# Graph attention on one core: batch 0's self features by seven block products, value blocks built in two groups of batches

## The chip, the cores and the metric

The kernel runs on one core of a Trainium2 chip. A core has five engines that run side by side, each with an instruction stream of its own: TensorE (PE, matrix products, with its weight loads shown as PEld), VectorE (DVE), ScalarE (ACT), GpSimd (POOL) and SyncE (SP), which in this kernel only issues DMAs. Transfers run on sixteen DMA engines. The metric is the device time of one execution in microseconds (us); lower is better.

## The reference

A graph attention layer, all in float32: B = 16 batches, N = 512 nodes, F = 512 features, H = 16 heads of 32 features, L = 11 edge labels, and only the first NG = 20 nodes of each batch serve as keys. What is computed, cut to its core:

```
row_zero  = v.sum(-1) == 0
q_exp     = where(row_zero, 0, q)                       # q: one vector per batch
self_feat = concat([v, q_exp]) @ W_self.T + b_self
output    = self_feat
for d in 0, 1:
    A    = adj if d == 0 else adj with its node axes swapped;  A = A[:, :, :20, :]
    cond = A.sum(-1);   vb = A @ w_bias + b_bias
    kv   = self_feat[:, :20]
    aff  = (self_feat @ Wq.T + bq) . (kv @ Wk.T + bk) / sqrt(32)       # per head
    aff  = where(cond > 0, aff, -9e15) + vb
    output += (softmax(aff) @ kv) @ Wout.T + bout                      # per head
result = v + relu(output)
```

## The kernel before, in words

Features lie on the partitions: a batch's input `x` is 4 chunks of 128 features x 512 nodes, and so is `sf`, its self feature. The query weights are folded into the keys, so that a batch's scores are one product of `sf` with a key tile `g` (4 chunks x 608 columns). Key 0 of each batch is taken off the others, so 19 key differences are left.

**Setup (to 91.4 us).** It makes the key rows, and then the key tiles of all 16 batches in 22 bursts of matmuls (`keys`, L674), n = 0 to 21. ACT and DVE empty each burst's two pairs of banks (L689, L691), and SP stores the keys in DRAM (`g_d`, `g1_d`). Behind the bursts from n = 4 on, PE does what the string `plan` says, one group of letters a burst: b and c are bias terms, v and w the value products (`values`, L649), n the flags of nodes whose row is not zero for batches 0 and 1, and s a step of batch 0's self feature. `values` copies its product to SBUF and stores it by POOL's DMAs in `vw_d` in DRAM.

**Batch 0's self feature before** (`self_feat`, L205) is a direct product: four quarters, each 4 x 2 x 4 matmul instructions over the four chunks of `x`. Three of the quarters are in the setup's plan, the fourth stands in the main loop between the scores of tiles 0 and 1.

**The self features of batches 1 to 15** are made while the batch before runs, by seven products of half-size blocks (`product`, L282, 32 matmul records each) instead of the eight of the direct way. They need sums of weight blocks (`weight_sums`, once, POOL) and sums of `x` blocks (`x_sum`, four a batch, POOL, L247). Products 1, 6, 7 and 4 add up in the banks `ps_a`; after each, DVE takes the banks' state to SBUF together with the flagged query term `nz` x `qw` (`partial`, L289). Products 2, 5 and 3 go to `ps_d` and `ps_c`, and DVE adds them to a partial (`joined`). A product that writes into `ps_a` must wait for the partial before it. In time: products 1 and 2 in tile 2 of the batch before, 6, 7 and 5 in tile 3, 4 and 3 in the batch's own tile 0.

**Main loop.** 16 batches of 4 tiles (`nt`) of 128 nodes. A tile: `scores` (PE, L365, into one of two pairs of banks `ps_s`), `weigh` (DVE: add the mask L379, maximum L383, subtract L387), `expo` (ACT, L392), `normal` (DVE sums L415 and L416, POOL multiply L417), `turn` (DVE transpose L424). `attend` (L435), `finish`, `residual` (L449) and `store` (L454) of batch b-1 run in tiles 2 and 3 of batch b. The masks come from the edge labels `adj`: `mask_mul` (ACT, L317), `mask_count` (DVE L322), `mask_sum` (DVE L328), `mask_spread` (ACT, L337), `full_add` (POOL, L344).

**The flags `nz` of batches 2 to 15.** `load_xn` (L111) brings the batch's rows two batches ahead, ACT sums them in tile 3 (`row_sum`, L169, four instructions), POOL compares with zero and a DMA stores 2 KB to `nz_d` (`row_mask`, L173 and L174), and a DMA spreads them over all partitions (`load_nz`, L178). `partial` is their user.

**Value blocks.** `attend` wants each batch's values as block-diagonal tiles `vd`, read from `bd_d` in DRAM (`load_values`, L139). `bd_d` (2 MB) is filled with zeros by one DMA (`clear_blocks`, batch 0, tile 1), and the values are copied into it from `vw_d` by twelve DMAs of 128-byte pieces (`blocks`, L162, batch 0, tile 2), each for all 16 batches.

**What sets the order.** The whole program is under a manual schedule: each engine runs its instructions in the order in which the code issues them, and a tile's buffers and semaphores make an engine wait. SP is one queue in order: a DMA that waits holds back all DMAs issued after it. `behind(dma, instruction)` ties a DMA to the end of an instruction of an engine, so that it is not issued earlier. Eight semaphores serve SP's DMAs in turn, so that a DMA also waits for the landing of the eighth before it.

## Time and profile before

| | us |
|---|---|
| three runs | 586.54, 587.45, 587.57 |
| median | 587.45 |
| the profiled execution | 586.05 |
| its span, first to last instruction | 583.9 |
| PE busy | 575.7 |
| DVE, ACT, POOL busy | 489.0, 395.6, 384.9 |
| main loop's first scores start | 91.38 |
| batch 1's, batch 2's first scores start | 122.48, 152.96 |

The rows are read in this way. A row of the costliest groups has line, engine, operation, output and input with their shapes, the number of instructions, then busy time and the mean of one in ns, and behind the bar's second part the idle time of the engine just before them with what ended most of it. A row of the chain or of the list of single instructions begins with the start and the duration in us. A row of waits has engine, tile and line, what was waited for, then the sum, the number and the longest. In a table by windows the columns are the stretch, its length, the busy time of PE, PEld, DVE, ACT and POOL with the number of instructions, the granted clock of PE, the busy share of the DMA engines and GB/s. A row on DMAs has the tiles, their number, the KB of each and the median us from issue to landing. SPq is SP's queue: start and duration of the issue.

### The profile page before, as it was taken

The numbers are of one execution on the slowest core, as the hardware profiler recorded it, in microseconds if no ns is written. First come the engines' busy times: TensorE is split into PE (matmuls) and PEld (weight loads), VectorE is DVE, ScalarE is ACT, GpSimd is POOL, SyncE is SP. The second block draws the span as 40 slices with busy tenths as digits, with TensorE's granted clock in tenths as the row PEclk, the third lists the DMA queues.
The fourth block names the chain that finished last, engine by engine and source line by source line (L and its number), as shares of the span: only waits on it lengthen the run. The fifth ranks groups of instructions, "written<-read, shape, count | busy, mean of one in ns | idle before, by whom it ended". The sixth has DMA issues, their size and how long they took to land.

```text
span 583.9 us, 30310 instructions
## 1 busy us (share of the span) xinstructions
PE 575.7 (99%) x13184; PEld 437.0 (75%) x13184; DVE 489.0 (84%) x783; ACT 395.6 (68%) x1162; POOL 384.9 (66%) x351
## 2 busy tenths in 40 slices
PE   9999999999999999999999999999999999999996
PEld 6654547887878787877878787787887878787873
DVE  0485565889898989899999999898989898989895
ACT  1334644586877777868686868687786877777671
POOL 2405663648778685858586777686868677776775
PEclk9999999999999999999999999999999999999999
DMA  8999899857766675757576767676676765664404
GB/s 303 388 407 311 331 377 320 273 123 213 209 197 196 185 214 169 217 167 217 168 214 171 214 171 212 177 199 188 199 202 187 199 198 172 199 199 114 144 15 146
DMA packets 103220, 124.14 MB, mean 213 GB/s; under 512 B 21712, under 2 KB 71920, under 8 KB 101040
## 3 DMA queue, kind: packets, MB, share of 16 engines
q1 hardware_dynamic: 101296, 119.79, 66.8%
q8 instruction: 104, 1.70, 1.3%
q0 software_dynamic: 672, 1.36, 1.0%
q10 hardware_dynamic: 1120, 1.06, 0.5%
q14 instruction: 28, 0.23, 0.2%
HBM read 82.30 MB, written 40.24 MB: 210 GB/s over the span
## 4 chain that ended last, share of the span: by engine, by line
PE 98%; DVE 0%; issue 0%; ACT 0%; DVEq 0%
PE ps_s L365 46%; PE ps_a L282 17%; PE ps_c L282 9%; PE ps_o L435 6%; PE ps_d L282 4%; PE ps_v L649 3%; PE ps_k L586 3%; PE ps_sf L205 2%; PE ps_kv L537 2%; PE ps_o L779 1%; PE ps_warm L496 1%; PE ps_nz L189 0%; PE ps_s L354 0%; PE ps_c L622 0%; PE ps_q L547 0%
## 5 line engine op out<-in xcount | busy, mean ns | idle before, releaser
L365 PEld LDWEIGHTS ps_s<-g,sf 128*32 128x32 f32 x8192 | 262.8, 110 | 20.9 <-issue 13.0
L365 PE MATMUL ps_s<-g,sf 128*32 128x152 f32 x8192 | 276.7, 293 | 0.5 <-ACT st L689 0.5
L337 ACT COPY both<-add 32x80 f32<-32x80 f32 x512 | 130.8, 256 | 53.8 <-DVE add L328 48.0
L417 POOL TENSOR_TENSOR s<-s,sm 128x640 f32<-128x640 f32 x63 | 80.4, 1276 | 94.2 <-DVE sm L416 68.2
L344 POOL TENSOR_TENSOR full<-cq,both 128x640 f32<-128x640 f32 x64 | 100.4, 1568 | 27.5 <-issue 21.3
L317 ACT ACTIVATE prod<-adj,wb_sb 128x80 f32<-128x80 int32 x330 | 112.4, 433 | 0.0
L392 ACT ACTIVATE s<-s 128x640 f32<-128x640 f32 x63 | 46.5, 738 | 64.1 <-DVE s L387 63.8
L449 POOL TENSOR_TENSOR o<-o,x 128x512 f32<-128x512 f32 x60 | 76.4, 1297 | 0.0
L379 DVE TENSOR_TENSOR full<-ps_s,full 128x608 f32<-128x608 f32 x63 | 48.8, 774 | 27.9 <-PE ps_s L365 22.6
L415 DVE TENSOR_REDUCE sm<-s 128x32 f32<-128x640 f32 x63 | 50.8, 806 | 9.5 <-ACT s L392 9.2
L282 PE MATMUL ps_a<-t,ws_s 128*32 128x246 f32 x960 | 55.4, 370 | 0.0
L383 DVE TENSOR_REDUCE ps_s<-full 128x32 f32<-128x640 f32 x63 | 52.2, 828 | 2.2
L424 DVE STREAM_TRANSPOSE wt<-s 128x640 f32<-128x640 f32 x63 | 52.7, 837 | 0.6 <-POOL s L417 0.6
L387 DVE TENSOR_TENSOR s<-full,ps_s 128x640 f32<-128x640 f32 x63 | 51.5, 817 | 1.1
L282 PEld LDWEIGHTS ps_a<-t,ws_s 128*32 128x32 f32 x960 | 31.6, 110 | 16.0
L328 DVE TENSOR_REDUCE add<-prod 128x80 f32<-128x960 f32 x32 | 36.8, 1150 | 6.2 <-ACT prod L317 4.4
L247 POOL TENSOR_TENSOR t<-x 128x492 f32<-128x492 f32 x30 | 34.6, 1153 | 9.5 <-DVE ps_s L383 5.4
L446 ACT ACTIVATE o<-o,bo 128x512 f32<-128x512 f32 x60 | 38.3, 713 | 0.6 <-DVE o L444 0.6
L435 PE MATMUL ps_o<-wt,vd 32*32 32x512 f32 (+5 forms) x816 | 36.7, 578 | 0.0
L444 DVE TENSOR_TENSOR o<-ps_o,sf 128x512 f32<-128x512 f32 x60 | 36.7, 668 | 0.0
L289 DVE SCALAR_TENSOR_TENSOR u<-nz,qw,ps_a 128x246 f32<-128x246 f32 x90 | 36.6, 448 | 0.0
L247 POOL TENSOR_TENSOR t<-x,t 128x492 f32<-128x492 f32 x30 | 34.5, 1150 | 2.3 <-DMA x<-in_xT 1.1
(239 smaller groups left out, 719.5 us busy)
## 6 DMA issues: line engine op xcount, KB each, us to landing
g_d<-st SPq DMA_DIRECT2D x16, 1064.0 KB, 5.9
g<-g_d SPq DMA_DIRECT2D x56, 304.0 KB, 3.6
out_T<-o SPq DMA_DIRECT2D x60, 256.0 KB, 3.3
x<-in_xT SPq DMA_DIRECT2D x56, 256.0 KB, 3.2
xn<-in_xn SPq DMA_DIRECT2D x52, 256.0 KB, 3.3
adj<-in_adj SPq DMA_DIRECT2D x56, 220.0 KB, 3.2
nz<-nz_d SPq DMA_DIRECT2D x14, 256.0 KB, 4.6
wk<-in_wkT SPq DMA_DIRECT2D x2, 1024.0 KB, 7.7
```

Source lines behind the costliest of these rows:

```text
L247: done["xsum"] = nc.gpsimd.tensor_sub(t, one, two)
L282: nc.tensor.matmul(to, lhs, x[:, k], start=start, stop=stop, skip_group_check=n != 2)
L317: nc.scalar.activation(p[:, :, l], a[:, :, l], AF.Identity, scale=wb_sb[:, l : l + 1])
L337: nc.scalar.copy(adds[b, h][bass.ts(a, R), :, g], add[r].rearrange("p (t m) -> p t m", t=2))
L344: done["full"] = nc.gpsimd.tensor_add(f, cqs[b].unsqueeze(1).to_broadcast(shape), adds[b, nt // 2][:, nt % 2].unsqueeze(2).to_broadcast(sh ...
L365: nc.tensor.matmul(to, sfs[b][:, k, bass.ds(nt * P + (2 * g + j) * R, R)], of, start=(onto is None and k == 0 and (whole or j == 0)), stop ...
L383: nc.vector.tensor_reduce(mx, f, AX.X, ALU.max)
L387: done["weigh"] = nc.vector.tensor_sub(s, f, mx.unsqueeze(3).to_broadcast(full))
L417: done["normal"] = nc.gpsimd.tensor_mul(s, s, sm.unsqueeze(3).to_broadcast(full))
L424: nc.vector.transpose(wts[b][:, nt], s.rearrange("p a h m -> p (a h m)"))
L435: nc.tensor.matmul(banks[a][bass.ds(at // 2 * DH, n * DH)].rearrange("p (t n) -> p t n", n=32), vd[r, bass.ds(at * DH, n * DH)], wt[r, :, ...
L449: nc.gpsimd.tensor_add(o[:, c], o[:, c], xs[b][:, c])
```

## The change

- Batch 0's self feature is made by the same seven products as that of the others, in the order 1, 2, 6, 7, 5, 4, 3, behind the last seven bursts of the setup (n = 15 to 21, letter p of the new `plan`). The direct `self_feat` and `self_copy` are gone, also from batch 0's tile 1. The sums it needs come earlier: `weight_sums` at n = 9 (13 before), batch 0's four `x_sum` at n = 11, into a tile of the `sf` pool. For batch 0 the products take their banks from the setup's rotating four.
- `partial` writes straight into `sf` in place of a tile `u` of its own, for all batches, and `joined` adds in place; so the new `sf` tile is taken in tile 2 (`new_self`) and not in tile 3.
- `vw_d` and `bd_d` are split: batches 0 to 3 and 4 to 15. Two stores of `values` become four. For the first group two clears (batch 0, tile 0) and twelve copies (batch 0, tile 2); for the second eight clears (four in each of batches 1 and 2, `clear_rest`) and twelve copies (six in each of batches 3 and 4, `spill`), one at a time between the loads.
- In batch 0, batch 1's `adj`, `cq` and keys and batch 2's `xn`, which were issued together (the keys ahead of the loop, the rest in tile 1), go one by one behind events from tile 0 to tile 3, among the twelve copies; `load_values(0)` comes inside tile 3.
- Batch 2's four row sums, all in batch 0's tile 3 before, come two after that tile's exponential and two after batch 1's `mask_mul(1, 1)`; its `row_mask` is moved behind batch 2's first `x_sum`.

```diff
-    vw_d = dram.tile([2, C, BM, P], F32, name="vw_d")
-    bd_d = dram.tile([C, B, 32, HL, 2, DH], F32, name="bd_d")
+    EARLY = 4
+    parts_of = ((0, EARLY), (EARLY, B))
+    vw_d = [dram.tile([2, C, (hi - lo) * NG, P], F32, name=f"vw_d{lo}") for lo, hi in parts_of]
+    bd_d = [dram.tile([C, hi - lo, 32, HL, 2, DH], F32, name=f"bd_d{lo}") for lo, hi in parts_of]
...
-    def clear_blocks(zero):
-
-        nc.sync.dma_start(
-            bd_d.rearrange("c b r e i g -> (c b r) (e i g)").rearrange("(n p) w -> p n w", p=P),
-            zero.unsqueeze(1).to_broadcast([P, C * B * 32 // P, HL * 2 * DH]),
-        )
-
-    def blocks():
-
-        bb = bd_d.rearrange("c b r e i g -> (c b) r e i g")
-        vv = vw_d.rearrange("d c (b m) (e g) -> d (c b) m e g", m=NG, e=HL)
+    def clear_first(n, ins):
+
+        rows = EARLY * 32
+        behind(nc.sync.dma_start(
+            bd_d[0][2 * n : 2 * n + 2].rearrange("c b r e i g -> (b r) c (e i g)"),
+            zero[:rows].unsqueeze(1).to_broadcast([rows, 2, HL * 2 * DH]),
+        ), ins)
+
+    def clear_rest(n, ins):
+
+        rows = (B - EARLY) * 8
+        to = bd_d[1][n // 2].rearrange("b r e i g -> (b r) (e i g)").rearrange("(n p) w -> p n w", p=rows)
+        behind(nc.sync.dma_start(
+            to[:, n % 2 * 2 : n % 2 * 2 + 2], zero[:rows].unsqueeze(1).to_broadcast([rows, 2, HL * 2 * DH])
+        ), ins)
+
+    def blocks(n):
+
+        found = []
+        bb = bd_d[n].rearrange("c b r e i g -> (c b) r e i g")
+        vv = vw_d[n].rearrange("d c (b m) (e g) -> d (c b) m e g", m=NG, e=HL)
         for e in range(HL):
             for i in range(2):
                 j = (e * S) // 32 + i
@@ -159,8 +171,13 @@
                     hi = min(e * S + (d + 1) * NG, 32 * j + 32)
                     if lo < hi:
                         m, r = lo - e * S - d * NG, lo - 32 * j
-                        nc.sync.dma_start(bb[:, r : r + hi - lo, e, i], vv[d, :, m : m + hi - lo, e])
-
+                        found.append((bb[:, r : r + hi - lo, e, i], vv[d, :, m : m + hi - lo, e]))
+        return found
+
+    def spill(n):
+
+        for _ in range(n):
+            nc.sync.dma_start(*copies.pop(0))
...
-            for k in ks:
-                for a in range(HL):
-                    nc.tensor.matmul(
-                        held[0][bass.ts(a, R), i * N // 2 : i * N // 2 + hi - lo],
-                        ws_v[:, k, bass.ds((2 * f + i) * P + a * R, R)], xs[b][:, k, lo:hi],
-                        start=(k == 0), stop=(k == C - 1),
-                    )
...
+        if b > 0:
+            t = xsum.tile([P, 2, HN], F32, tag=f"t{n}", name=f"t{b}_{n}")
+        else:
+            if n == 1:
+                held[0] = sfp.tile([P, C, N], F32, tag="sf", name="t0")
+            t = held[0][:, n - 1, : 2 * HN].rearrange("p (k n) -> p k n", k=2)
+        sums[b, n] = t
...
-            parts[b, "a"] = [bank(f"ps_a{b}_{i}", i) for i in range(2)]
+            parts[b, "a"] = [bank(f"ps_a{b}_{i}", i if b else None) for i in range(2)]
...
-    def partial(b, n, f, l, to=None):
-
-        if to is None:
-            to = us[b, n] = xsum.tile([P, 2, HN], F32, tag=f"u{n}", name=f"u{b}_{n}")
+    def partial(b, f, l):
+
+        to = block(b, f, l)
...
-    def joined(b, n, key, f, l):
+    def joined(b, key, f, l):
 
         done["joined"] = nc.vector.tensor_add(
-            block(b, f, l), parts[b, key][:, : 2 * HN].rearrange("p (i n) -> p i n", i=2), us.pop((b, n))
+            block(b, f, l), parts[b, key][:, : 2 * HN].rearrange("p (i n) -> p i n", i=2), block(b, f, l)
...
+                        edge = EARLY * NG
+                        for n, lo, hi in ((0, 0, edge), (1, edge, rows)) if t == 0 else ((1, 0, rows),):
+                            nc.gpsimd.dma_start(
+                                vw_d[n][d, :, bass.ds(t * P + lo - n * edge, hi - lo)].rearrange("c r w -> r c w"),
+                                v[bass.ds(i * rows + lo, hi - lo)].rearrange("p (c w) -> p c w", c=C),
+                            )
...
+            def block_product(n):
+
+                product(0, n)
+                f, args = {
+                    1: (partial, (0, 0, 0)), 2: (joined, (0, "d", 0, 0)), 6: (partial, (0, 0, 1)),
+                    7: (partial, (0, 1, 1)), 5: (joined, (0, "c", 1, 1)), 4: (partial, (0, 1, 0)),
+                    3: (joined, (0, "c", 0, 1)),
+                }[n]
+                f(*args)
...
-                "s": [
-                    (self_step, (0, f, h, i, k)) for f, h in ((0, 0), (1, 0), (0, 1))
-                    for i in range(2) for k in range(C)
-                ],
+                "p": [(block_product, (n,)) for n in (1, 2, 6, 7, 5, 4, 3)],
...
-            plan = "bvv vv vv ccw vv ns ssss sssw vv vv ssss ssss vv vv nww ssss ssss".split()
+            plan = "bvv vvc vvc vvn vv vvw vv vv w w wn p p p p p p p".split()
...
+                if n == 9:
+                    row_sums(1)
+                    weight_sums()
                 if n == 11:
-                    row_sums(1)
-                if n == 13:
-                    weight_sums()
+                    new_self(0)
+                    for i in range(1, 5):
+                        x_sum(0, i)
...
-                if b == 0 and nt == 1:
-                    load_adj(1, 0)
-                    load_cq(1)
-                    clear_blocks(zero)
-                    load_adj(1, 1)
-                    load_xn(2, 0)
-                    load_xn(2, 1)
-                if b == 0 and nt == 2:
-                    blocks()
-                if nt == 2 and last or nt == 3 and b == 0:
+                if nt == 2 and last:
...
+                        if b == 1:
+                            for j in range(2, 4):
+                                row_sum(2, j)
...
-                        if more:
+                        if more and b > 1:
                             row_mask(b + 1)
...
+                        if b in (1, 2):
+                            clear_rest(4 * b - 4, done["masks"])
+                        elif b in (3, 4):
+                            copies = copies or blocks(1)
+                            spill(1)
...
+                    if b == 0:
+                        load_adj(1, 0, done["spread"], slice(0, 1))
...
+                    if b == 0:
+                        clear_first(0, done["mixed"])
+                        load_adj(1, 0, done["weigh"], slice(1, 2))
+                        clear_first(1, done["exp"])
...
+                        if b in (1, 2):
+                            if b == 1:
+                                row_mask(2)
+                            clear_rest(4 * b - 3, done["xsum"])
+                        elif b in (3, 4):
+                            spill(1)
...
-                        self_feat(0, 1, 1)
...
+                    if b == 0:
+                        load_keys(1, range(1), done["full"])
...
+                    if b == 0:
+                        load_adj(1, 1, done["normal"], slice(0, 1))
+                        copies = blocks(0)
+                        spill(3)
+                        load_keys(1, range(1, 2))
+                        load_adj(1, 1, None, slice(1, 2))
+                        spill(3)
+                        load_keys(1, range(2, 3))
+                        spill(2)
+                        load_xn(2, 1, None, slice(0, 1))
+                        spill(2)
+                        load_keys(1, range(3, C))
+                        spill(2)
+                    elif more:
...
+                        new_self(b + 1)
+                    s = weigh(b, nt, pair, (lambda: partial(b + 1, 0, 0)) if more else None)
...
-                    new_self(b + 1)
-                    joined(b + 1, 1, "d", 0, 0)
+                    joined(b + 1, "d", 0, 0)
...
-                    if b + 2 < B:
+                    if 0 < b < B - 2:
                         for j in range(4):
                             row_sum(b + 2, j)
                     normal(*prev)
-                    partial(b + 1, 2, 0, 1)
+                    if b == 0:
+                        load_xn(2, 1, done["xsum"], slice(1, 2))
+                        load_values(0, done["normal"])
+                    partial(b + 1, 0, 1)
...
+                    if b == 0:
+                        for j in range(2):
+                            row_sum(2, j)
```

80 lines of the change are left out of this document (32 added, 48 removed).

## The prediction

> **What bounds the kernel now.** I read the page's busy times first, then the waits of PE, then the chain that ended last, piece by piece.
>
> ```profile
> PE 575.7 (99%) x13184; PEld 437.0 (75%) x13184; DVE 489.0 (84%) x783; ACT 395.6 (68%) x1162; POOL 384.9 (66%) x351
> ```
>
> ```profile
> PE ps_s L365 <- ACT st L689: 0.5, 1, 0.5
> ```
>
> PE is the bound from its first matmul to the tail: 575.7 of 583.9 us. So a microsecond of matmul removed is a microsecond gained, and a new wait of PE is lost at once unless PE finds it covered. PE's waits are nearly nothing; this one and another, shown in part 2, lie in the changed stretch. Everything else in this change (DMAs, ACT, POOL, DVE) costs only what it makes PE wait. The chain around the change, start, length, what (x32 is one block product, or half of one 236-wide self_feat step):
>
> ```profile
> 91.38 4.34 PE ps_s L365 x128
> 95.72 3.45 PE ps_sf L205 x64
> 107.44 1.66 PE ps_a L282 x32
> 122.48 4.13 PE ps_s L365 x128
> 142.17 1.66 PE ps_a L282 x32
> 152.96 4.13 PE ps_s L365 x128
> ```
>
> **Part 1, seven products in place of self_feat.** All of batch 0's L205 matmuls go, and seven products of 32 records come into the last seven setup bursts (n = 15 to 21).
>
> ```profile
> L205 PE MATMUL ps_sf<-x,ws_v 128*32 128x256 f32 x128 | 7.5, 380 | 0.0
> L205 PE MATMUL ps_sf<-x,ws_v 128*32 128x236 f32 x128 | 7.4, 366 | 0.0
> ```
>
> ```profile
> 56.88 0.71 PE ps_g(1, 3, 1, 0, 2)0_552 L674 x4
> ...
> 58.27 1.73 PE ps_sf L205 x32
> ...
> 60.99 1.33 PE ps_sf L205 x24
> 62.32 1.01 PE ps_v L649 x4
> ```
>
> Removed: 7.5 + 7.4 = 14.9 us. Added: 7 x 1.66 = 11.6. But 1.66 is a product among like matmuls. In a burst, 32 records of 236 columns take 1.73, where 1.66 x 236/246 would be 1.59; entering from the key matmuls costs 0.14. So 11.6 + 7 x 0.14 = 12.6, and the term is **-2.3 us** (-3.3 if entry is free, -1.7 if time goes by columns alone, 27552/31488 of 14.9).
>
> **Part 2, PE's two waits.** The 0.5 us before the first scores is a wait for ACT to empty the last key burst's bank. In the new order a 1.66 us product stands between them, which covers 0.5: **-0.5**. The other wait, placed by the chain:
>
> ```profile
> 109.51 0.73 issue
> ```
>
> ```profile
> 107.00:111.00 4.00, 3.27 (x72) 2.14 (x64) 3.93 (x8) 3.36 (x12) 2.79 (x2) 1.00 1.05 390
> ```
>
> No semaphore ends it; it falls where the DMA engines are full (share 1.05, 390 GB/s). The change takes 1.5 of the 2 MB zero-fill out of that stretch. I take **-0.7**; if it is not DMA, 0.
>
> **Part 3, the setup's hold-ups.** The key burst at 56.88 lasted 1.39 us to its next step, the one after it (58.27 + 1.73 to 60.99) 0.99: there DVE emptied the bank late. A second such burst starts at 63.33, where the value step ends. The new order trades these two (some 0.8 together) for others. Bursts 12 to 14 have one 64-row value step (1.01 us) of cover against DVE's emptying:
>
> ```profile
> 67.75 1.17 DVE L691 TENSOR_SCALAR st<-ps_g(2, 1, 1, 1, 2)1_658 128x304 f32<-128x304 f32 x2 [1.72 <-PE ps_g(2, 1, 1, 1, 2)1_658 L674]
> ...
> 77.22 1.06 DVE L322 TENSOR_REDUCE cond<-adj 128x80 f32<-128x880 int32 x1
> ```
>
> That is 0.2 late, twice; and in burst 17 the mask count (1.06) stands, with the joined add, ahead of the emptying: about 0.4. So 0.8 against 0.8, and I take **0** (-0.9 to +0.9). The partials that DVE adds there (0.84 us a pair, row below) and the joins run under the 1.66 us products; a product that adds into the same banks comes two bursts later, or one key burst (1 us) later for 6 then 7. If DVE ran a microsecond later, product 7 would wait for product 6's partial.
>
> **Part 4, batch 0 without its 3.45 us of cover.** That self_feat step stood between the scores of tiles 0 and 1; POOL and DVE worked under it. Now PE reaches the end of tile 2's scores earlier and POOL does not:
>
> ```profile
> 100.63 1.27 POOL L417 TENSOR_TENSOR s<-s,sm 128x640 f32<-128x640 f32 x1 [2.02 <-DVE sm L416]
> ...
> 104.17 1.57 POOL L344 TENSOR_TENSOR full<-cq,both 128x640 f32<-128x640 f32 x1
> ```
>
> ```profile
> 107.87 0.73 DVE L379 TENSOR_TENSOR full<-ps_s,full 128x608 f32<-128x608 f32 x1
> 108.63 0.83 DVE L383 TENSOR_REDUCE ps_s<-full 128x32 f32<-128x640 f32 x1
> 109.37 0.84 DVE L289 SCALAR_TENSOR_TENSOR u<-nz,qw,ps_a 128x246 f32<-128x246 f32 x2
> ```
>
> The setup grows (12.6 for the 11.45 us of L205 it held), so the first scores start near 92.4, not 91.38. POOL's run to tile 2's mask (ended 105.74) ends a microsecond later, at 106.7; PE's three score tiles end at 92.4 + 3 x 4.2 = 105.0 (107.44 before). DVE then needs 0.73 + 0.83 + half of 0.84 = 2.0 until product 6 may write its bank: 108.75. PE, after two products (3.3), is there at 108.3: **+0.45** (0 to +1). The rest of batch 0 I follow in the same way without a wait. PE then enters batch 1 by 2.3 + 0.5 + 0.7 - 0.45 = 3.05 us sooner.
>
> **Part 5, the DMAs.** The change takes the 2 MB clear and twelve 64-block copies from SP in batch 0, and puts in two small clears and twelve copies with a quarter of the pieces, among the loads of batch 1, now each behind an event. SP before:
>
> ```profile
> 124.74 2.45 SPq L139 DMA_DIRECT2D vd<-bd_d  x4
> 127.23 1.84 SPq L105 DMA_DIRECT2D x<-in_xT  x4
> 129.18 0.38 SPq L174 DMA_DIRECT2D nz_d<-nz  x1
> ...
> 134.26 0.33 SPq L178 DMA_DIRECT2D nz<-nz_d  x1
> ...
> 138.39 1.80 SPq L111 DMA_DIRECT2D xn<-in_xn  x4
> ```
>
> ```profile
> L162 SPq DMA_DIRECT2D bd_d<-vw_d x12: 611/716/1692, 108.6 to 119.9; - x12
> ```
>
> ```profile
> xn<-in_xn SPq DMA_DIRECT2D x4, 256.0 KB, 6.2
> ...
> nz<-nz_d SPq DMA_DIRECT2D x1, 256.0 KB, 3.9
> ...
> nz_d<-nz SPq DMA_DIRECT2D x1, 2.0 KB, 5.0
> ```
>
> ```profile
> xn<-in_xn SPq DMA_DIRECT2D x52, 256.0 KB, 3.3
> ...
> nz_d<-nz SPq DMA_DIRECT2D x14, 2.0 KB, 3.5
> ```
>
> The first three are landing times in the stretch 128 to 150, the last two the page's medians.
>
> New order: POOL's normal of tile 1 ends at 106.7 + 1.27 = 108.0 and releases nineteen issues: twelve copies (0.6 each, the smallest of before), two adj and two xn (0.46, by 1.84/4), three key loads (0.6, as a copy): 10.9, to about 118.9. Keys of the last chunk go at 117.6 and land after about 3.3 (the page's 256 KB loads, below), at 121; the second half of batch 1's first scores needs them near 122, so I cost this at nothing with a microsecond to spare. The last copy (at 118) lands at 121.3 to 122; then vd (2.45), batch 2's x (second piece out by 124.9, landed 128.1). Here comes the new wait: batch 2's row mask is moved behind POOL's first x sum of batch 2.
>
> ```profile
> 124.15 0.25 POOL L173 TENSOR_SCALAR nz<-rs 128x4 f32<-128x4 f32 x1
> ...
> 130.80 1.05 POOL L247 TENSOR_TENSOR t<-x 128x492 f32<-128x492 f32 x1 [4.10 <-DMA x<-in_xT]
> ```
>
> The sum ends at 129.1, the mask at 129.4, its store goes at 129.7 and lands 3.5 to 5.0 us later; SP stands in that wait, and everything behind it too (the nz load, four cq, two adj, two added clears of 0.46, four xn). The nz load, let go at 133.2 to 134.7, lands at 137.1 to 138.6. Its user, DVE's partial, must be half done when product 6 of batch 2 is due, 142.17 - 3.05 = 139.1, so must start at 138.7: no room is left, and I take 0.2 (0 to 0.7). The xn loads start 4.1 us after the nz load before, now 5.05: at 138.3 to 139.8, in the old clock 141.3 to 142.8, 2.9 to 4.4 us late. ACT has them first in a queue that ends at PE:
>
> ```profile
> 144.31 0.63 ACT L169 ACTIVATE xn<-xn 128x512 f32<-128x512 f32 x1 [1.06 <-DMA xn<-in_xn]
> ...
> 147.43 4.26 ACT L337 COPY both<-add 32x80 f32<-32x80 f32 x16 [0.35 <-DVE add L328]
> ```
>
> ```profile
> 153.61 0.75 DVE L289 SCALAR_TENSOR_TENSOR sf<-nz,qw,ps_a 128x246 f32<-128x246 f32 x2
> ```
>
> Row sums, spreads, exp, DVE's sum, then the partial whose first half was ready at 154.0; PE wanted it at 152.96 + 2.06 = 155.0. Slack: 0.35 at the spreads and 1.0 here, 1.35. So 1.6 to 3.0 if xn again lands in 6.2, and none if in 3.3; taken 1.3, the middle of 0 and the mean of those. Together **+1.5** (0 to +3).
>
> The Trainium skill (DMA: Bandwidth & Descriptors, "Anatomy of one DMA") gives a DMA a fixed cost of about 2.0 us, most of it the receipt of the write, fitted on GpSimd's path; by it the 2 KB store would land 3 us sooner than the 5.0 of the row, part 5 would cost nothing, and the sum would be -3.05. This trace does not agree: 5.0 here, 3.5 in the median, on SP's queue.
>
> **Edits costed at nothing.** The second group's eight clears and twelve copies lie in batches 1 to 4, where SP mostly waits:
>
> ```profile
> SPq L454 <- POOL o L449: 56.1, 60, 5.5
> ```
>
> Without that cover each copy (0.6 to 0.7) would push the next load, and the first to be late would be the xn loads again. Partials written straight into sf and the earlier new_self keep their number and lengths. Two more value stores on POOL and the earlier weight sums lie before burst 15, where POOL has no user that waits. Two of batch 2's four row sums (1.4 us, half of 144.31 to 147.1 in the row above) now follow the exp of batch 0's last tile and two follow batch 1's mask products, so batch 1's mask sum and first softmax come that much later; PE has a whole tile's scores (4.1) in hand there, in the other bank.
>
> **Sum.** -2.3 - 0.5 - 0.7 + 0 + 0.45 + 1.5 = -1.55 us. The profiled execution took 586.05 us (span 583.9 and 2.15 around it), 1.4 below the median of three, 587.45; against the median the sum gives 585.9.
>
> **Rivals.**
> - No give-back: nz and xn land in time. For it: landings of 3.3 us when the engines are not full; against: the 6.2 and 5.0 rows. 587.45 - 3.05 = 584.4.
> - Nearly no change: the 0.73 stays (-0.5 - 2.3 = -2.8 of gains) and part 5 costs its full 3: 587.45 - 2.8 + 0.45 + 2.2 = 587.3. For it: nothing proves that the 0.73 is DMA's.
> - Slower, by SP's queue in batch 0: if the copies take 0.9 us each in place of 0.6 (the longest of before took 1.7), everything behind them is 3.6 us later; the last keys land at 124.6 and PE waits 2.6 in batch 1's first scores, then for nz and xn some 2 more. -3.05 + 2.6 + 2.0 = +1.55: 589.0. It decides from about 0.75 us a copy on. For it: twelve of before came 1.0 apart (108.6 to 119.9). Against: four times the pieces then, on full engines.
>
> **How the numbers follow.** Forecast 585.9: chance 0.40. No give-back: 0.19. Nearly none: 0.24. Slower: 0.17. What can be told from no change is 0.2%, 1.2 us: faster is below 586.3, slower above 588.6. Of the forecast I count a tenth to "same", so faster 0.36 + 0.19 = 0.55, same 0.04 + 0.24 = 0.28, slower 0.17. Its own range is 584.9 to 586.8; the range for all reaches from 583.9 (no give-back with free entry into the bursts) to 588.9, just short of the slower rival.
>
> **What would show it.** Right: no L205 rows; seven products of 1.7 to 1.8 us ahead of the first scores at 92 to 93; no 0.5 before them; batch 1's product 4 (120.82 before) near 117.8; the nz store later than 128.5, and a PE wait in batch 2's first scores (second half) or before batch 1's last product 6, behind DVE's partial. Wrong: a PE wait for a key load in batch 1 (SP's queue), product waits in bursts 17 to 21, or a batch 3 or 4 longer than the 30.48 us from one batch's first scores to the next's (122.48 to 152.96).

## The result and the profile after

The changed kernel is slower: 590.22 us in the median of seven runs (588.13 to 592.64) against 586.54 us in the median of seven for the kernel before beside it, a ratio of 1.0062 (95% interval 1.0045 to 1.0079). The forecast was 585.9, with 583.9 to 588.9 as its range. The profiled execution took 591.38 us with a span of 589.6. A trace is of one execution, and the executions of one kernel lie 1.4 to 6.5 us apart in this case; so kernels are compared by their medians, and a trace tells how time was lost in one execution.

The page of the changed kernel, its busy times and the clock granted to PE in 40 slices:

```profile
PE 578.1 (98%) x13152; PEld 438.1 (74%) x13152; DVE 491.3 (83%) x786; ACT 395.9 (67%) x1162; POOL 390.4 (66%) x357
...
PEclk9999999999899999999999999999999999999999
```

PE's busy time is still the time, but one slice shows a granted clock of 0.8. The next view shows PE's waits (name, line, releaser; sum, number, longest):

```profile
PE ps_s L358 <- DVE sf L282: 3.4, 1, 3.4
PE ps_a L276 <- issue: 1.1, 2, 0.6
```

The wait for ACT ahead of the first scores is gone, as forecast. A wait of 3.4 us for DVE's partial is new. PE's instructions in time show where the 5.7 us between the two spans arise. First four rows of the kernel before: product 1 of batch 1, product 1 of batch 2, and the scores of batch 2's first and second tile (start, duration, then engine, line and operation):

```profile
107.25 1.84 PE L282 MATMUL ps_a<-x,ws_v 128*32 128x246 f32 x32
...
138.67 1.84 PE L282 MATMUL ps_a<-x,ws_v 128*32 128x246 f32 x32
...
152.78 4.32 PE L365 MATMUL ps_s<-g,sf 128*32 128x152 f32 x128
...
158.57 4.32 PE L365 MATMUL ps_s<-g,sf 128*32 128x152 f32 x128
```

The same view of the changed kernel:

```profile
93.09 12.58 PE L358 MATMUL ps_s<-g,sf 128*32 128x152 f32 x384
105.49 1.84 PE L276 MATMUL ps_a<-x,ws_v 128*32 128x246 f32 x32
...
109.62 1.87 PE L276 MATMUL ps_a<-t,ws_s 128*32 128x246 f32 x32 [0.62 <-issue]
...
118.74 1.87 PE L276 MATMUL ps_a<-t,ws_v 128*32 128x246 f32 x32
120.40 4.70 PE L358 MATMUL ps_s<-g,sf 128*32 128x152 f32 x128
...
137.15 1.84 PE L276 MATMUL ps_a<-x,ws_v 128*32 128x246 f32 x32
...
151.06 1.23 PE L276 MATMUL ps_a<-t,ws_v 128*32 128x246 f32 x17 [0.46 <-issue]
...
152.33 2.36 PE L358 MATMUL ps_s<-g,sf 128*32 128x152 f32 x58
158.11 4.28 PE L358 MATMUL ps_s<-g,sf 128*32 128x152 f32 x64 [3.42 <-DVE sf L282]
162.16 2.68 PE L276 MATMUL ps_c<-x,ws_s 128*32 128x246 f32 x32
164.67 4.31 PE L358 MATMUL ps_s<-g,sf 128*32 128x152 f32 x128
```

PE is 1.76 us ahead at batch 1's product 1 (105.49 for 107.25) and still 1.52 ahead at batch 2's (137.15 for 138.67). Then it loses 7.6 us between batch 2's product 4 and its second tile, whose scores start 6.10 us late (164.67 for 158.57). It stands still for 0.46 us in product 4 with no releaser, and for 3.42 us in the middle of batch 2's first scores. After that the second half of the scores takes 4.28 us (half of the last row's 4.31 would be 2.2) and product 3 takes 2.68 in place of 1.84. The stretches in a table (length, busy times of the five engines, then the granted clock, the DMA share and GB/s) say why:

```profile
156.00:160.00 4.00, 1.89 (x32) 1.44 (x36) 3.40 (x6) 4.00 (x12) 3.42 (x4) 0.63 0.39 137
160.00:164.00 4.00, 4.00 (x60) 2.61 (x56) 2.66 (x3) 2.17 (x9) 2.62 (x3) 0.52 0.43 108
```

By the trace's clock records PE ran at 0.50 of its clock from 157.03 to 163.86; the 0.63 and 0.52 of the two rows are means over four microseconds each. Of the 7.6 us, 0.46 and 3.42 are the two waits, and 2.8 is the half clock (worked out below). The other 0.9 lies in product 4 and the first half of the scores, which took 4.63 us without the gap and 3.74 before; what stretched them was not separated. Nothing of note follows: from batch 3 to batch 15 the two kernels' batches start 5.8 to 6.1 us apart.

SP's queue in the same batch (issue start, duration) shows the chain that I had forecast, only longer:

```profile
128.56 0.42 SPq L157 DMA_DIRECT2D bd_d<-zero  x1
...
131.09 0.38 SPq L191 DMA_DIRECT2D nz_d<-nz  x1
131.53 0.42 SPq L157 DMA_DIRECT2D bd_d<-zero  x1
135.66 0.32 SPq L195 DMA_DIRECT2D nz<-nz_d  x1
136.07 2.67 SPq L124 DMA_DIRECT2D cq<-cq_d  x4
138.79 0.42 SPq L157 DMA_DIRECT2D bd_d<-zero  x1
139.26 1.97 SPq L119 DMA_DIRECT2D adj<-in_adj  x2
141.27 0.43 SPq L157 DMA_DIRECT2D bd_d<-zero  x1
141.80 1.89 SPq L113 DMA_DIRECT2D xn<-in_xn  x4
```

SP's list of waits between 130 and 142 us has two entries, the store's landing and the mask on POOL:

```profile
SPq L195 <- DMA nz_d<-nz: 3.7, 1, 3.7
SPq L119 <- POOL nz L190: 1.8, 1, 1.8
```

ACT's row sums (L186), spreads and exponential, and what DVE does after them:

```profile
146.94 0.63 ACT L186 ACTIVATE xn<-xn 128x512 f32<-128x512 f32 x1 [4.42 <-DMA xn<-in_xn]
...
150.89 0.63 ACT L186 ACTIVATE xn<-xn 128x512 f32<-128x512 f32 x1 [1.48 <-DMA xn<-in_xn]
...
151.52 4.24 ACT L330 COPY both<-add 32x80 f32<-32x80 f32 x16
155.79 0.74 ACT L385 ACTIVATE s<-s 128x640 f32<-128x640 f32 x1
```

```profile
156.56 0.82 DVE L408 TENSOR_REDUCE sm<-s 128x32 f32<-128x640 f32 x1 [6.14 <-ACT s L385]
...
157.68 0.75 DVE L282 SCALAR_TENSOR_TENSOR sf<-nz,qw,ps_a 128x246 f32<-128x246 f32 x2
```

The nz store goes out at 131.09 (129.18 before), the nz load at 135.66 (134.26), the xn loads from 141.80 (138.39). The last row sum starts at 150.89 (146.36 before), and behind it stand 16 spreads, the exponential, DVE's sum and the partial that PE waits for.

### The profile page after: what moved, and what is told of

Same layout as the page of the kernel before. It is cut to its first block, busy times and chain, and to the rows that moved or that the text cites. A ratio compares the mean times of both kernels' runs of the same rounds, so it can differ in the third digit from the quotient of the medians.

```text
span 589.6 us, 30303 instructions
## 1 busy us (share of the span) xinstructions
PE 578.1 (98%) x13152; PEld 438.1 (74%) x13152; DVE 491.3 (83%) x786; ACT 395.9 (67%) x1162; POOL 390.4 (66%) x357
## 4 chain that ended last, share of the span: by engine, by line
PE 88%; DVE 5%; ACT 3%; issue 2%; DMA 1%; POOL 1%; DVEq 0%; ACTq 0%; POOLq 0%
PE ps_s L358 40%; PE ps_a L276 16%; PE ps_c L276 8%; PE ps_o L428 6%; PE ps_d L276 4%; PE ps_k L579 3%; PE ps_v L639 3%; PE ps_kv L530 2%; ACT both L330 1%; DMA xn<-in_xn 1%; PE ps_o L774 1%; DVE sm L408 1%; DVE full L372 1%; ACT prod L310 1%; DVE ps_s L376 1%
## 5 line engine op out<-in xcount | busy, mean ns | idle before, releaser
L358 PE MATMUL ps_s<-g,sf 128*32 128x152 f32 x8192 | 279.8, 294 | 3.6 <-DVE sf L282 3.4
L276 PE MATMUL ps_a<-t,ws_s 128*32 128x246 f32 x1024 | 59.2, 371 | 0.6 <-issue 0.6
L282 DVE SCALAR_TENSOR_TENSOR sf<-nz,qw,ps_a 128x246 f32<-128x246 f32 x128 | 51.6, 443 | 0.7 <-PE ps_a L276 0.7
L276 PEld LDWEIGHTS ps_a<-t,ws_s 128*32 128x32 f32 x1024 | 33.2, 110 | 18.6 <-POOL s L410 1.1
L241 POOL TENSOR_TENSOR t<-x 128x492 f32<-128x492 f32 x32 | 36.9, 1152 | 9.8 <-DVE full L372 6.2
L186 ACT ACTIVATE xn<-xn 128x512 f32<-128x512 f32 x56 | 34.5, 618 | 6.6 <-DMA xn<-in_xn 6.6
L241 POOL TENSOR_TENSOR t<-x,t 128x492 f32<-128x492 f32 x32 | 36.8, 1151 | 1.3
```

Source lines behind the costliest of these rows:

```text
L241: done["xsum"] = nc.gpsimd.tensor_sub(t, one, two)
L276: nc.tensor.matmul(to, lhs, x[:, k], start=start, stop=stop, skip_group_check=n != 2)
L358: nc.tensor.matmul(to, sfs[b][:, k, bass.ds(nt * P + (2 * g + j) * R, R)], of, start=(onto is None and k == 0 and (whole or j == 0)), stop ...
```

## The experiments

All times are beside runs of the kernel before on the same chip; a ratio below 1 is faster than the kernel before.

**The two halves of the change apart.** `products_only` is the changed kernel with one value block, the 2 MB clear, the twelve large copies, batch 1's loads, and batch 2's row sums and row mask put back as they were:

```diff
-    vw_d = [dram.tile([2, C, (hi - lo) * NG, P], ...) for lo, hi in parts_of]
+    vw_d = dram.tile([2, C, BM, P], F32, name="vw_d")
...
+                if b == 0 and nt == 1:
+                    load_adj(1, 0); load_cq(1); clear_blocks(zero); load_adj(1, 1); load_xn(2, 0); load_xn(2, 1)
+                if b == 0 and nt == 2:
+                    blocks()
...
-                            for j in range(2, 4):
-                                row_sum(2, j)
```

> The kernel before with the seven block products for batch 0, the partials straight into sf and the new order of the setup, but with one value block, one 2 MB clear, twelve large copies, the loads of batch 1 and the row sums of batch 2 as before. Theory A: the products' gain as the changed kernel's trace shows it ahead of batch 2 (1.5 to 1.9 us) and nothing given back: 584.6 to 585.2, ratio 0.997. PE's 0.73 us without a releaser, which the forecast gave to the zero fill, stays near 107 to 110. If the products themselves cost (a rival in which the setup's longer steps are the loss): 587 or more.

`blocks_only` is the complement: everything else of the change on top of the kernel before, which keeps its `self_feat`.

> The complement: the kernel before with the value blocks in two groups, batch 1's loads behind events and batch 2's split row sums and moved mask, but batch 0's self feature by the direct product as before. Theory A: the flags are as late as in the changed kernel by SP's queue, but PE comes 1.5 us later, so it waits some 2 to 3 us in batch 2's first scores; with the clock falling 5 us are lost, without 2.5: 589 to 592. If the loss needs both parts (a PE that runs ahead): 586.5 to 587.5. The 0.73 us near 109 is gone if the zero fill caused it.

Measured: products only 584.56 us beside 587.88, ratio 0.9948 (0.9931 to 0.9966); value blocks only 591.81, ratio 1.0068 (1.0044 to 1.0092). Both times came out as expected. So the products are worth 3.3 us in the medians, and all of the loss comes with the other half. The trace of `products_only` is of an execution of 586.56 us, above that kernel's other five, with 1.1 us of PE's wait for an opening load and 1.9 without a releaser; so it doesn't show where the 3.3 us are, of which the changed kernel's trace accounts for 1.8. The sum of the two halves (+0.16%) is less than the whole change (+0.62%). In `blocks_only` PE comes later and waits only 0.58 us for the partial, but it also stood still for 2.09 us without a releaser, at the end of batch 1, where the DMA engines were full. This fits a PE that waits away what it gains ahead of a moment that SP sets. It isn't shown apart from the clock, which fell in the changed kernel's trace and not in that of `blocks_only`.

**Where in that half.** Four kernels move the two suspects. `mask_first` is the changed kernel with

```diff
                     if more:
+                        if b == 1:
+                            row_mask(2)
                         x_sum(b + 1, 1)
```

> The changed kernel with one edit: batch 2's row mask stands on POOL before batch 2's first x sum and not behind it. Theory A (the flags' chain on SP): in the changed kernel the nz store goes out at 131.1, the nz load at 135.7, the xn loads at 141.8 to 143.3, and PE waits 3.4 us in batch 2's first scores and then runs at half its clock for some 6 us. POOL stands idle before that x sum (3.6 us, for x), so the mask moves to about 127, the store to about 128.7, the nz load to about 133.3 and the xn loads to about 139.5; the row sums end near 149 in place of 151.5, PE waits about 1 us or less and its clock stays full. Time about 585 us, 5 below the changed kernel, a ratio to the kernel before of 0.997. Theory B (the four added clears of 0.4 us on SP in batch 1 and the DMA load around them, not the mask): the nz load moves but the xn loads hardly, at most 1 us less wait, clock still falling: 588.5 to 590. Theory C (the loss has no fixed place, a clock that varies from run to run): as the changed kernel, 590.

`clears_b2` leaves the mask and issues the second group's eight clears in batch 2, two at each place, and none in batch 1 (one of the four places; the others are alike):

```diff
                         if b in (1, 2):
-                            clear_rest(4 * b - 4, done["masks"])
+                            if b == 2:
+                                clear_rest(0, done["masks"])
+                                clear_rest(1, done["masks"])
```

> The changed kernel with only the clears moved: all eight clears of the second group in batch 2, none in batch 1; the row mask stays behind the x sum. So far the mask alone brought the changed kernel from 1.0062 to 0.9998 of the kernel before, mask and clears together to 0.9972. If the two are one chain on SP's queue whose delays add up (theory A and B as one), the clears alone give about what both give beyond the mask, and a little more, since the wait that they shorten is longer and a shorter wait also spares time at half clock: 0.998 to 1.001, 586 to 588. If the mask's place is what decides and the clears only trim: 1.004 to 1.006.

`both` has the two edits together.

> The same edit of the row mask, and all eight clears of the second group issued in batch 2 (two at each of the four places), none in batch 1. Theory A: like the run with the mask alone within 0.7 us, about 584.7, since 1 us of slack is already there. Theory B: this one gains 1.5 to 5 us more than the mask alone, because SP loses four issues of 0.4 us ahead of the xn loads. Theory C: 590.

`flags_late` is `products_only` with the mask's move alone (`row_mask(2)` behind `x_sum(2, 1)`).

> The kernel with the products alone (0.9948 of the kernel before) with one edit: batch 2's row mask behind batch 2's first x sum, as in the changed kernel, while its row sums, clears and copies stay as before. It tests the move of the mask by itself. If the mask's move is enough to make xn late: the store goes out some 3 us later, SP stands behind it, the xn loads come 2 to 3 us later, PE waits 1 to 2 us in batch 2's first scores and may run at half clock: 586 to 589. If it needs SP's other new work too, the slack covers it: 584.6, no change.

Measured ratios: mask first 0.9998 (0.9983 to 1.0013), clears in batch 2 0.9971 (0.9960 to 0.9982), both 0.9972 (0.9960 to 0.9984), the mask's move on top of the products 0.9964 (0.9951 to 0.9976). Either edit brings the kernel level with the kernel before or below it; neither reaches the products' 0.9948. `mask_first` (587.75 us) lies between what its theories A and B forecast; `clears_b2` gained more than forecast. The clears weigh more: without them in batch 1 the mask's place makes no difference, and on top of the products the mask's move costs little or nothing (0.9964 for 0.9948, with intervals that overlap). With the clears out of batch 1 SP's queue reads

```profile
131.81 0.38 SPq L191 DMA_DIRECT2D nz_d<-nz  x1
134.68 0.33 SPq L195 DMA_DIRECT2D nz<-nz_d  x1
135.10 2.56 SPq L124 DMA_DIRECT2D cq<-cq_d  x4
137.77 0.84 SPq L119 DMA_DIRECT2D adj<-in_adj  x2
138.66 1.85 SPq L113 DMA_DIRECT2D xn<-in_xn  x4
```

The store is even later (131.81), but the nz load follows it after 2.9 us and not after 4.6, and the xn loads start 4.0 us after that load and not 6.1. They are 3.1 us earlier in time, and 3.9 sooner behind the store. Of the 3.9, 1.7 is the store's quicker landing, 0.9 the two clears between the loads, and 1.1 an adj issue that takes 1.4 us in the changed kernel and 0.4 here (the rows of two adj issues, 1.97 and 0.84). SP's list above shows no wait there for any landing but the store's, so the semaphores that SP's DMAs share held nothing back for long. Why the store lands later and that issue takes longer with the clears around is not shown. A table over the traces, in us. "Last row sum" is the start of the last of ACT's row sums in batch 1 (of batch 3's rows), "product 1" that of batch 2's product 1 on PE, "lag" the one less the other:

| kernel | nz store | first xn load | last row sum | product 1 | lag | PE's wait for the partial |
|---|---|---|---|---|---|---|
| before | 129.18 | 138.39 | 146.36 | 138.67 | 7.69 | 0 |
| products only | 132.08 | 140.87 | 147.65 | 139.93 | 7.72 | 0 |
| clears in batch 2 | 131.81 | 138.66 | 145.75 | 137.85 | 7.90 | 0 |
| both | 130.35 | 140.67 | 147.92 | 138.86 | 9.06 | 0 |
| keys first (below) | 128.08 | 138.39 | 145.79 | 136.34 | 9.45 | 0.22 |
| mask late on products | 133.91 | 140.88 | 148.30 | 138.50 | 9.80 | 0.45 |
| value blocks only | 132.69 | 143.05 | 151.37 | 139.12 | 12.25 | 0.58, after 2.09 without a releaser |
| mask first | 130.73 | 142.67 | 150.80 | 138.66 | 12.14 | 2.01 |
| changed kernel | 131.09 | 141.80 | 150.89 | 137.15 | 13.74 | 3.42 |

The three kernels with clears in batch 1 (the last three rows) have lags of 12.1 to 13.7 us, the six without them 9.8 at most, wherever the mask stands. The wait begins between 9.06 and 9.45 and grows with the lag. The slack is thus about 1.6 us (9.3 less 7.7), close to the 1.35 that I read, or 2.2 by the last row (13.74 less 7.69, less PE's 3.42 and 0.46); the lag is 6 us more than before. Of this, 1.5 us is PE's own lead. `mask_first` got little of what its edit was to bring. The trace is of an execution of 590.18 us, in which PE is 1.5 us behind the changed kernel's at product 1; counted from there the store went out 1.9 us sooner, where 2.4 was expected, but the nz load only 0.4 sooner, since it took 6.0 us from store to load. Between 132 and 134 us the DMA share was 0.95 there, and 0.50 with the clears in batch 2.

**The keys.** `mask_first` and its sisters show a wait that I had costed at nothing:

```profile
PE ps_s L358 <- DMA g<-g_d: 1.0, 1, 1.0
```

`keys_first` is `both` with batch 1's last key chunks ahead of most copies:

```diff
-                        spill(3)
                         load_keys(1, range(2, 3))
-                        spill(2)
-                        load_xn(2, 1, None, slice(0, 1))
-                        spill(2)
+                        spill(3)
                         load_keys(1, range(3, C))
-                        spill(2)
+                        load_xn(2, 1, None, slice(0, 1))
+                        spill(6)
```

> The changed kernel with mask first and clears in batch 2 (0.9972), and batch 1's last two key chunks issued before six and three of the copies and not behind ten. The runs showed PE waiting 0.5 to 1.0 us for a key load in batch 1's first scores, which I had costed at nothing. If that wait is SP's queue, it goes, 0.5 us are won, and the copies land no later than before: about 585.7. If the later copies hold up the value blocks, SP and with it the flags: no gain or a loss of up to 2 us.

Measured: 583.62 us beside 586.85, ratio 0.9948 (0.9936 to 0.9959). The key wait is gone, the span of the profiled execution is 581.5 us (583.9 before), and the whole change, with three edits to the place of its DMAs, is 0.5% faster than the kernel before. That is 2 us better than expected, of which the key wait explains 1.0 at most, and it is no better than the products alone.

**The value blocks, mended, by themselves.** `blocks_mended` gives `blocks_only` the same three edits.

> The kernel with the value blocks in two groups and the direct product for batch 0 (1.0068 of the kernel before), with the three edits that brought the changed kernel from 1.0062 to 0.9948: mask first, clears in batch 2, keys ahead of most copies. If the loss of that part was only SP's queue in batches 0 and 1, it is gone, and what is left is the gap that the 2 MB fill caused (0.7 us in the kernel before): 0.998 to 1.000, 585.5 to 587. If the part costs by itself (its clears and copies in batches 1 to 4): 1.002 or more. With the products' 0.9948, the first would also say that the products carry nearly all of the best version's gain.

Measured: 588.53, ratio 1.0028 (1.0009 to 1.0047): worse than the 0.998 to 1.000 of SP's queue alone. Two more kernels put the clears one at a time into batches 2 and 3 and the second group's copies, two at a time, into batch 4:

```diff
-                        if b in (1, 2):
-                            if b == 2:
-                                clear_rest(0, done["masks"])
-                                clear_rest(1, done["masks"])
-                        elif b in (3, 4):
+                        if b in (2, 3):
+                            clear_rest(4 * b - 8, done["masks"])
+                        elif b == 4:
                             copies = copies or blocks(1)
-                            spill(1)
+                            spill(2)
```

> The mended value-block part with the direct product (1.0028 of the kernel before, where 0.998 to 1.000 was expected), with its eight clears one at a time in batches 2 and 3 and not two at a time in batch 2, and its last twelve copies two at a time in batch 4. In the mended kernel's trace the loss lies in batches 2 and 3 (0.4 us behind at batch 2's third tile, 1.6 at batch 4's first) with no named wait of PE, at a DMA share of 0.94 to 0.98 where the kernel before has 0.68 to 0.84. If the loss is the two clears at a time (DMA engines full, instructions late as with the fills), it falls to 0.998 to 1.000; if it is the part's bytes and issues wherever they stand, it stays at 1.002 to 1.004.

> The best version so far of the whole change (0.9948) with the same spreading of clears and copies. Its trace shows no loss in batches 2 and 3, so the first reading expects little: 0.993 to 0.995. If the doubled clears did cost there in some executions, 0.992.

Both became slower, against both forecasts: 592.06, ratio 1.0077 (1.0052 to 1.0102), and 590.20, ratio 1.0040 (1.0017 to 1.0064). The first one's trace runs level with that of the kernel before through batches 2 and 3, so the single clears cost nothing there, where the doubled ones had cost `blocks_mended` 1.9 us. The loss of both traces lies in batch 4, where the copies are (6.8 and 4.4 us). SP and PE of the first of the two:

```profile
229.57 1.20 SPq L180 DMA_DIRECT2D bd_d<-vw_d  x2
230.86 1.94 SPq L119 DMA_DIRECT2D adj<-in_adj  x2
232.85 1.23 SPq L180 DMA_DIRECT2D bd_d<-vw_d  x2
234.18 0.54 SPq L113 DMA_DIRECT2D xn<-in_xn  x1
234.76 1.62 SPq L180 DMA_DIRECT2D bd_d<-vw_d  x2
236.48 1.03 SPq L113 DMA_DIRECT2D xn<-in_xn  x2
```

```profile
245.64 0.47 PE L382 MATMUL ps_s<-g,sf 128*32 128x152 f32 x8 [0.94 <-DMA g<-g_d]
...
251.82 3.80 PE L382 MATMUL ps_s<-g,sf 128*32 128x152 f32 x64 [3.32 <-DVE sf L306]
```

Each pair of copies holds SP for 1.2 to 1.6 us ahead of a load, PE waits 1.3 us for keys and 3.32 us for the same partial, and its clock falls for 3.4 us. That is the changed kernel's fault made again in another batch, by added DMAs alone and with no mask moved.

**What PE's waits without a releaser are.** `fills` adds three DMAs that write zeros to a spare tile, otherwise unused:

```diff
+                if (b, nt) in fills:      # (5, 0), (8, 1), (11, 3)
+                    nc.scalar.dma_start(spare_d[fills[b, nt]]..., zero.unsqueeze(1).to_broadcast(...))   # 2 MB
```

> The kernel before with three more 2 MB fills of a spare DRAM tile from ScalarE's queue, in the steady batches 5 (tile 0), 8 (tile 1) and 11 (tile 3); nothing reads them. It asks what PE's waits without a releaser are (0.73 us near 109 in the kernel before, 1.4 and 0.5 with the products alone, 2.1 near 151 with the value blocks alone). In six traces each of them ends 2.3 to 2.6 us after the start of a 16 KB transfer on the instruction queue, in a stretch where the DMA engines are full. If they are late instruction fetches under full DMA engines, new gaps of 0.4 to 2 us without a releaser appear on PE within some 8 us of a fill wherever such a transfer falls into it, and none in the other steady batches. If the fill is harmless to fetches, waits appear only behind named loads, or none.

Measured: 592.18 us in one execution, 5.3 above the median before. PE's list of waits has four new gaps without a releaser, 4.1 us in all, the only ones of that kind in the trace:

```profile
PE ps_s L367 <- issue: 3.5, 3, 1.4
PE ps_c L284 <- issue: 0.6, 1, 0.6
```

The instruction queue's 16 KB transfers ahead of each such gap, from the traces (us):

```
kernel          transfer starts   PE stands still      end less start
before               107.73       109.51 to 110.24         2.51
products only        103.91       105.14 to 106.55         2.64
products only        110.38       112.28 to 112.76         2.38
blocks only          150.69       151.15 to 153.24         2.55
changed kernel       148.75       150.61 to 151.06         2.31
mask first           150.17       152.11 to 152.51         2.34
fills                247.44       249.05 to 249.70         2.26
fills                252.55       254.36 to 255.07         2.52
fills                353.04       354.05 to 355.39         2.35
fills                465.15       466.06 to 467.51         2.36
```

Ten gaps, each over 2.3 to 2.6 us after such a transfer began, and in the two microseconds ahead of each transfer the DMA share was 0.97 to 1.11. The last gap begins 3.4 us after its fill had landed, at a share that was still 1.05. Of all 22 gaps without a releaser of 0.15 us or more in the fourteen traces, between the opening loads and the tail, sixteen end 2.2 to 2.8 us after such a transfer. The other six, each 0.6 us near 109 in kernels with the whole change, have none in the five microseconds before and are taken for the wait of part 4 below. Full engines alone are not enough: only about one in ten of the transfers that began at a share of 1.0 or more was followed by such a gap. It is an inference that PE waited for its next instructions; that full DMA engines bring such gaps about is shown by the fills.

**Whether a wait by itself lowers the clock.** `ladder` delays the row sums in six batches of the kernel before by idle ScalarE copies:

```diff
+                        for _ in range(late.get(b, 0)):    # {3: 6, 5: 8, 7: 9, 9: 10, 11: 12, 13: 14}
+                            nc.scalar.copy(pad, zero)
                         for j in range(4):
                             row_sum(b + 2, j)
```

> The kernel before with idle ScalarE copies (0.4 us or so each, 256 columns into a spare tile) ahead of the row sums in tile 3 of batches 3, 5, 7, 9, 11 and 13: 6, 8, 9, 10, 12 and 14 of them. They delay spreads, exponential and the last partial as the late xn loads did, with no DMA moved. It asks whether a PE wait by itself brings the half clock of the changed kernel (3.4 us of wait, then 0.50 to 0.57 granted for 6.4 us, some 3 us more). If the clock falls by the length of the wait: full after waits under some 2 us, half after waits of 3 us and more, and the batch then loses the wait plus 2 to 3 us. If the half clock had another cause (DMA load, power), it stays full at every step and the batch loses only the wait. Slack by the trace is 1.35 us, so the first step should wait about 1 us and the last about 4.

Measured: 598.96 us in one execution, 12.0 above the median before, of which the named waits are 8.4; the rest is not explained. PE waited 0, 0.58, 1.00, 1.29, 2.31 and 3.18 us, so the slack in these batches is about 2.5 us (14 copies of 0.406 are 5.7, less 3.18). The clock stayed full in all six batches, at 3.18 us of wait too:

```profile
533.58 2.40 PE L367 MATMUL ps_s<-g,sf 128*32 128x152 f32 x64 [3.18 <-DVE sf L291]
```

The 64 records of this row take 2.40 us, those of the changed kernel's second half took 4.28. So the length of the wait doesn't decide, against what I expected. The times of the falls do: in every trace the stretches of full and half clock last a whole number of 3.413 us, but for the last stretch, which the end of the trace cuts (6.83 = 2 x 3.413 in the changed kernel, one in `mask_first` and in each of the two spread kernels). Cut into such windows, the one before the fall was idle for 2.34 of 3.41 us in the changed kernel (154.69 to 157.03) and for 2.01 in `mask_first` (156.01 to 158.02); the ladder's 3.18 us fell across a boundary as 1.88 and 1.30, and the clock held. The clock records of all fourteen traces, with their tails, bear this out: each of the 18 falls follows a window with 2.01 to 3.41 us idle, and no window idle for 1.88 us or less is followed by one. A window at half clock that was idle for 1.08 us (the changed kernel's first) was followed by another; those idle for 0.23 or less were followed by the full clock.

## Why the prediction was wrong

The steps in order.

- **Part 1** (-2.3) measured -1.76 by the two traces. The seven products took 12.48 us from start to start, within 0.12 of the forecast (six at 1.80, the last at 1.68). But L205 took only 14.24: 10.79 in the setup and 3.45 in batch 0. I had added the busy times of its two groups, 7.5 and 7.4, and they overlap at the edges. The -1.7 that I gave for time by columns alone is 1.9 by its own numbers.
- **Part 2.** The 0.5 is right. The 0.7 was gone from its place, and that full DMA engines bring such gaps about is now shown, but "I take -0.7" was too simple: a gap can go wherever full DMA engines meet an instruction transfer. The changed kernel has one at 151 (0.46).
- **Part 3** (0) held: the hold-ups of bursts 12 to 14 came as described (bursts of 1.30 and 1.39 us in place of 0.98, and 0.2 before the first of them).
- **Part 4** (+0.45) measured 0.62, at 109.0 to 109.62, behind DVE's partial. At batch 1's product 4 PE was 1.87 us ahead (118.74; 120.61 before in the same view), where 3.05 was forecast. Of the 1.2 missing, 0.54 is part 1, 0.17 this wait, 0.25 was lost before 39 us, among the opening loads, and 0.14 the two bias score steps that the new plan keeps apart (2 x 0.65 for 1.16).
- **Part 5** is the step that failed. The chain was the right one, wait for wait (mask, store, nz load, xn, row sums, spreads, exponential, partial, PE), and nz itself was in time. But its wait was taken as "1.3, the middle of 0 and the mean of those" (the middle is 1.15), and PE waited 3.42 us there, with 7.6 lost in all around it. By the old clock the xn loads were not 2.9 to 4.4 us late but 4.9 (141.80 + 1.5 - 138.39), although PE's lead was 1.5 and not 3.05; in the kernel's own time they went out 2.0 to 3.5 us later than forecast. Three pieces were missing. First, the store was 1.4 us late (131.09 for 129.7): in batch 0 the twelve copies took 0.70 us each and not 0.6, and the second x load, which the mask now waits for, went out at 126.64 and not by 124.9. Second, from the nz load to the xn loads it took 6.1 us and not 5.05. I had counted the two clears there at 0.46 each and nothing else; taking all four out of the batch brought the xn loads 3.1 us forward. So the edit costed at nothing, "SP mostly waits", was not free: SP's waits are not slack when a chain with 1.6 us to spare runs through the same queue. Third, the last xn load landed after 7.6 us and not 6.2, so the row sums were 6 us late, and 6 less the slack is about the wait and the gap that were measured.
- **The half clock** had no term at all. It added 2.8 us in the trace (6.56 from 158.11 to 164.67, where 2.07 + 1.66 = 3.73 is the full clock's time). The mean granted clock of each execution says how often. It is 0.996 to 0.999 in the 24 executions of the kernel before that ran beside `mask_first`, 0.992 to 0.995 in five of the changed kernel's seven (0.996 and 0.999 in the others), 0.997 to 0.999 in eleven of the twelve of `mask_first`, and 0.994 in the one that was profiled. So the fall is usual in the changed kernel, and the trace of `mask_first` is the exception among its executions. The Trainium skill (TensorE: Matmul & The Clock Gate, "What's actually happening") says that the array goes to half clock after an idle window of about 3.4 us, counted in free-running windows. The traces agree on the window (3.413 us) and on its running free (the clock first rises 4.6 to 6.9 us after a trace's start, by the run); they differ on "idle", since a window busy for 1.4 of 3.41 us was enough.

Of the rivals, "slower, by SP's queue in batch 0" came nearest in time (589.0). Its place was only a small part: the first scores of batch 1 are 0.36 longer in the changed kernel (4.70 for 4.34), and the wait for keys is up to 1.0 in its sisters. Its "nz and xn some 2 more" was the main one. That its 589.0 lies near the 590.22 is luck: the 2.6 for keys did not come, and the half clock, which it lacks, did. "No give-back" is what `products_only` does: 0.9948 of 587.45 is 584.4, the time that was worked out for it, though its trace does not show the terms. Two figures of the working do not follow from their own terms: "nearly no change" names part 5's full 3 but adds 2.2 (with 3 it gives 588.1), and the range's lower end, no give-back with free entry, is 583.4 and not 583.9.

Open: why the doubled clears of batch 2 cost the mended value blocks their 0.28% alone and cost nothing beside the products. In the first trace PE has no named wait after the setup; single steps are stretched in batches 2 and 3, most of them where the DMA share is 0.90 to 0.98 (0.68 to 0.84 before), one `attend` (3.24 us for 2.58 before) at 0.74. Late instructions could look like this, but no run separates it. Open too: where the 3.3 us of the products come from beyond the 1.8 of the trace.

## What to carry to other kernels

On a queue that issues in order, an idle queue isn't slack: look for the tightest chain through it (here a 2 KB store, the load that waits for it, and the loads behind both), and put nothing between its links. An engine's lead ahead of data that another queue times is not a gain until that data is earlier too. And where the bound engine may stand still, cost the wait with what follows it: here 2.0 us or more of standing within one 3.41 us window was followed by one or two windows at half clock, each worth up to 1.7 us (half of 3.41).

## What the runs showed of the hardware that I had not expected

- In all fourteen traces PE's granted clock changes only on a grid of 3.413 us, and it fell at 2.01 us or more idle in a window and held at 1.88 or less.
- With the DMA engines full (shares of 1.0 to 1.1), PE stood still ten times for 0.4 to 2.1 us without a semaphore, until 2.3 to 2.6 us after an instruction transfer began. The Trainium skill (Runtime: NRT & Kernel Launch, "Instruction fetch mechanics") calls the cost of crossing a 16 KiB block mostly hidden; if these gaps are that cost, which is the inference above, it was not always hidden here once the DMA engines were full.
- The same 2 KB store let the load behind it go after 2.9 us (with the clears in batch 2) to 6.0 us (`mask_first`). I had 3.5 to 5.0, from one trace.
